# A gate's logits with the weights stationary and a group's features moving

## The chip, the cores and the metric

The kernel runs on one core of one Trainium2 chip. Its time is the device time of one execution in microseconds, the median of several runs. The core has five engines that matter here: TensorE (PE; its weight loads have rows of their own, PEld), VectorE (DVE), ScalarE (ACT), GpSimd (POOL), and SyncE (SP), which only issues transfers.

## The reference, cut to what matters

One layer of a graph network over 3125 nodes with 512 features. A two-layer graph attention and a linear attention are added to the input; then comes a mixture of eight experts of which each node uses two. The change touches the logits of the expert gate alone.

```python
def _L0_ffn_ref(x, Wg, bg, W1, b1, W2, b2):
    ...
    logits = xf @ Wg + bg
    probs = jax.nn.softmax(logits, axis=-1)
    _, top_idx = jax.lax.top_k(probs, TOP_K)
    mask = jnp.any(top_idx[:, :, None] == jnp.arange(NUM_EXPERTS)[None, None, :], axis=1)
    comb = probs * mask.astype(probs.dtype)
    out = jnp.zeros_like(xf)
    for e in range(NUM_EXPERTS):
        h = jax.nn.gelu(xf @ W1[e] + b1[e])
        y = h @ W2[e] + b2[e]
        out = out + comb[:, e:e + 1] * y
...
x = x + _L0_ffn_ref(_layernorm(x, axis=-1)[None], L0_ffn_Wg, ...)[0]
```

`xf` is 3125 x 512, `Wg` is 512 x 8, `W1[e]` is 512 x 128, `W2[e]` is 128 x 512, all in float32.

## The kernel before, in words

The two attention layers fill most of the time. After them, `last` (line 981) does the layer norms, the gate and the experts. Its nodes come in 25 tiles of 128 (`TILES`; the last one has 53), and these in seven groups of four tiles (`FGROUPS`; the last group is the tile of 53 alone). The group of 53 is first, then the other one that stayed on the chip (`STAY`; its features appear as `xg` in the profile), then the five others (`xT`).

For a group, the generator `gates(t0, k)` (line 987) makes the routing weights in steps divided by `yield`:

- `ps`, lines 998 to 1003: features turned to rows of nodes (TensorE), copied into `yall` by ScalarE, row statistics on VectorE.
- lines 1005 to 1021: first layer norm, the sum with `bt` and `bx`, which GpSimd gathers from memory, and statistics again.
- lines 1023 to 1035: the second layer norm gives `z`; `to_features` (line 450) turns `z` to features in four transposes into one PSUM tile `tr` (two buffers), and copies it into `xT` by VectorE and ScalarE in turn (lines 446 and 448). Then, tile by tile, the gate's product: four matmuls (one per chunk of 128 features, `NP` = 4) with the features of 128 nodes stationary and the 8 columns of `wgt` moving, into `pg` of 128 x 8 (PSUM, one buffer). VectorE adds the bias `bgt`, which is spread over 128 partitions, and writes `prob` (line 1035).
- lines 1038 to 1058: softmax over the 8 experts and a ranking, on VectorE but for one Exp on ScalarE.
- lines 1060 to 1066: the weights turned to `combT` (line 1063; `pc` shares the buffer of `pg`).

`expert_sums(t0, k, ahead)` (line 1068) uses them: `pb` (line 1074) has the second biases, then for each of eight experts `ph` (line 1080, four chunks of 512 columns), a Gelu on ScalarE into `hT` (line 1083), `py` (line 1087, four tiles) and a multiply-add into `yall` on VectorE (line 1089). After each expert it takes one step of the next group's `gates` (line 1091), so that the gate of a group is made in the time of the group before. At its end the rows go to memory through GpSimd's queue (line 1095). The first group's gate runs ahead of everything.

The program's order gives each instruction its priority; the order in which an engine takes them is set when the kernel is built, by which of them can be ready. In every engine they then run in that order. A float32 matmul appears as two instructions in the profile, a transpose as one.

`load_experts` (line 964) loads the experts' weights, `wgt`, `bgt` and `gt` on SP's queue, while the last attention layer ends.

Of the kernel before, what the change touches and what calls it, by code (L numbers as in the profile page):

```python
# [8 lines left out]
F32 = mybir.dt.float32  # L9
BF16 = mybir.dt.bfloat16  # L10
I32 = mybir.dt.int32
AF = mybir.ActivationFunctionType
# [9 lines left out]
NP = H // 2  # L22
# [4 lines left out]
NX = 8  # L27
FX = 128
GT = 4
# [4 lines left out]
P = 128  # L34
# [43 lines left out]
def rows_by_partition(ap, r0, n):  # L78

    return bass.AP(tensor=ap.tensor, offset=ap.offset + r0 * ap.shape[-1],  # L80
                   ap=[[0, n], [1, ap.shape[-1]]])
# [328 lines left out]
def listed_layers(ctx: ExitStack, tc: tile.TileContext, rows,  # L410
# [4 lines left out]
    nc = tc.nc  # L415
# [34 lines left out]
    def to_features(pool, tag, o, rows_sb, n, copy=None):  # L450

        ps = pool.tile([128, 512], F32, name="tr", tag=tag)
        for c in range(NP):
            nc.tensor.transpose(ps[:, c * n:(c + 1) * n], rows_sb[:n, c * 128:(c + 1) * 128],
                                ident[:n, :n])
        (copy or evacuate)(o, ps[:, :NP * n].rearrange("p (c r) -> p c r", c=NP))
# [8 lines left out]
    def row_stats(pool, rows_in, mv_t):  # L465
        n = rows_in.shape[0]
        st = pool.tile([P, 6], F32, name="row_st", tag="row_st", bufs=4)
        nc.vector.bn_stats(st[:n], rows_in)
        nc.vector.bn_aggr(mv_t, st[:n])

    def node(t):
        return rec[:TILES[t][1], t, 0:1]
# [491 lines left out]
    def load_experts(fp):  # L964
        w1t = fp.tile([128, NX, NP, FX], F32, name="w1t")
        w2t = fp.tile([FX, NX, D], F32, name="w2t")
        for e in range(NX):
            nc.sync.dma_start(w1t[:, e], w1[e].rearrange("(c p) f -> p c f", p=128))
            nc.sync.dma_start(w2t[:, e, :], w2[e])
        b2t = fp.tile([NX, D], F32, name="b2t")  # L970
        nc.sync.dma_start(b2t, b2)
        wgt = fp.tile([128, NP, NX], F32, name="wgt")
        nc.sync.dma_start(wgt, wg.rearrange("(c p) e -> p c e", p=128))
        bgt = fp.tile([P, NX], F32, name="bgt")
        nc.sync.dma_start(bgt, rows_by_partition(bg, 0, P))
        gt = fp.tile([P, D], F32, name="gt")
        nc.sync.dma_start(gt, rows_by_partition(rows, ROW_G, P))
        return w1t, w2t, b2t, wgt, bgt, gt


    def last(xT, w1t, w2t, b2t, wgt, bgt, gt):
        with tc.tile_pool(name="fin", bufs=1, reuse_waits="tile") as fp, \
# [4 lines left out]
            def gates(t0, k):  # L987


                tiles = TILES[t0:t0 + k]  # L990
                mv = fp.tile([P, GT, 2], F32, name="mv1", bufs=2)
                mv2 = fp.tile([P, GT, 2], F32, name="mv2", bufs=2)
                prob = fp.tile([P, GT, NX], F32, name="prob", bufs=3)
                nc.vector.memset(mv, 1.0)
                nc.vector.memset(mv2, 1.0)
                nc.vector.memset(prob, 0.0)
                for i, (t, n) in enumerate(tiles):
                    ps = pp.tile([P, 512], F32, name="ps", tag="tr")
                    for c in range(NP):
                        nc.tensor.transpose(ps[:n, c * 128:(c + 1) * 128],  # L1000
                                            xT[:, c, t * P:t * P + n], ident)
                    nc.scalar.copy(yall[:n, t, :], ps[:n])
                    row_stats(fp, yall[:n, t, :], mv[:n, i, :])
                yield
                inv = fp.tile([P, GT], F32, name="sd_y", bufs=2)
                nc.scalar.activation(inv, mv[:, :, 1], AF.Sqrt, bias=epst)
                nc.vector.reciprocal(inv, inv)
                for i, (t, n) in enumerate(tiles):
                    bt = fp.tile([P, D], F32, name="bt", bufs=4)
                    bx = fp.tile([P, D], F32, name="bx", bufs=3)  # L1010
                    for o, held_in in ((bt, base), (bx, xb)):
                        nc.gpsimd.indirect_dma_start(  # L1012
                            out=o[:n], out_offset=None, in_=held_in[:, :],
                            in_offset=bass.IndirectOffsetOnAxis(ap=node(t), axis=0))
                    nc.gpsimd.tensor_add(bt[:n], bt[:n], bx[:n])
                    y = yall[:n, t, :]
                    nc.vector.scalar_tensor_tensor(y, y, mv[:n, i, 0:1], gt[:n],
                                                   op0=OP.subtract, op1=OP.mult)
                    nc.vector.scalar_tensor_tensor(y, y, inv[:n, i:i + 1], bt[:n],  # L1019
                                                   op0=OP.mult, op1=OP.add)  # L1020
                    row_stats(fp, y, mv2[:n, i, :])
                yield
                sd = fp.tile([P, GT], F32, name="sd_z", bufs=2)
                nc.scalar.activation(sd, mv2[:, :, 1], AF.Sqrt, bias=epst)
                nc.vector.reciprocal(sd, sd)
                for i, (t, n) in enumerate(tiles):
                    z = fp.tile([P, D], F32, name="z", bufs=3)
                    nc.vector.tensor_scalar(z[:n], yall[:n, t, :], mv2[:n, i, 0:1], sd[:n, i:i + 1],
                                            op0=OP.subtract, op1=OP.mult)
                    to_features(pp, "tr", xT[:, :, t * P:t * P + n], z, n)  # L1030
                    pg = pp.tile([P, NX], F32, name="pg", bufs=1)
                    for c in range(NP):
                        nc.tensor.matmul(pg[:n], lhsT=xT[:, c, t * P:t * P + n], rhs=wgt[:, c, :],  # L1033
                                         start=(c == 0), stop=(c == NP - 1))
                    nc.vector.tensor_add(prob[:n, i, :], pg[:n], bgt[:n])
                yield

                m = fp.tile([P, GT], F32, name="pm", bufs=2)
                wide = [P, GT, NX]
                nc.vector.tensor_reduce(m, prob, AX.X, OP.max)  # L1040
                nc.vector.tensor_sub(prob, prob, m[:, :, None].to_broadcast(wide))
                nc.scalar.activation(prob, prob, AF.Exp)
                nc.vector.tensor_reduce(m, prob, AX.X, OP.add)
                nc.vector.reciprocal(m, m)
                nc.vector.tensor_mul(prob, prob, m[:, :, None].to_broadcast(wide))

                rank = fp.tile(wide, F32, name="rank", bufs=2)
                nc.vector.memset(rank, 0.0)
                for e in range(NX):
                    more = fp.tile(wide, F32, name="more", bufs=2)  # L1050
                    pe = prob[:, :, e:e + 1]
                    nc.vector.tensor_tensor(more[:, :, :e + 1], pe.to_broadcast([P, GT, e + 1]),
                                            prob[:, :, :e + 1], OP.is_gt)
                    if e + 1 < NX:
                        nc.vector.tensor_tensor(more[:, :, e + 1:], pe.to_broadcast([P, GT, NX - 1 - e]),
                                                prob[:, :, e + 1:], OP.is_ge)
                    nc.vector.tensor_add(rank, rank, more)
                nc.vector.scalar_tensor_tensor(prob, rank, 1.5, prob, op0=OP.is_lt, op1=OP.mult)
                yield
                combT = fp.tile([NX, GT * P], F32, name="combT", bufs=2)  # L1060
                pc = pp.tile([NX, 512], F32, name="pc", tag="pg", bufs=1)
                for i, (t, n) in enumerate(tiles):
                    nc.tensor.transpose(pc[:, i * P:i * P + n], prob[:n, i, :], ident[:n, :n])
                w = (k - 1) * P + tiles[-1][1]
                nc.vector.tensor_copy(combT[:, :w], pc[:, :w])
                gated[t0] = prob, combT

# [33 lines left out]
            for _ in gates(*groups[0]):  # L1101
                pass
            for i, g in enumerate(groups):
                expert_sums(*g, gates(*groups[i + 1]) if i + 1 < len(groups) else iter(()))
# [3 lines left out]
    for l in range(L):  # L1108
# [10 lines left out]
        with tc.tile_pool(name=f"x{l}", bufs=1, reuse_waits="tile") as fx:  # L1119
            parts = [stay[g] if g in STAY else fx.tile([128, NP, GT * P], F32, name=f"xT{g}")  # L1120
                     for g in range(len(FGROUPS))]
            xT = Groups(parts)
# [601 lines left out]
```

## Time and profile before

| what | us |
|---|---|
| median of the 3 runs shown (2830.23, 2837.37, 2837.75) | 2837.37 |
| the profiled execution | 2804.75 |
| its span, first to last instruction | 2803.0 |
| PE busy in the span | 2398.1 (86%) |
| DVE busy | 2054.1 (73%) |
| ACT busy | 1406.5 (50%) |
| POOL busy | 1414.4 (50%) |
| mean granted TensorE clock | 0.911 of full |

`last` begins at about 2321 us of the span. PE in the span's last five stretches of a hundred:

| stretch | PE busy | clock |
|---|---|---|
| 2300 to 2400 | 76.79 | 0.73 |
| 2400 to 2500 | 99.36 | 0.98 |
| 2500 to 2600 | 99.93 | 0.95 |
| 2600 to 2700 | 99.85 | 0.98 |
| 2700 to 2803 | 92.44 | 0.94 |

A line of the profile's groups gives line, engine, operation, the tiles written and read, the shape (for TensorE: rows times columns of the stationary operand, then the moving one), the count, and then busy time and the mean of one. In a timeline a line has the start, the time from the first start to the last end, and what ran. The end of a matmul is modelled and lies behind the start of the next, so what TensorE pays for a run of matmuls is the distance from its start to the start of what follows. "Clock" is the share of TensorE's full clock that the chip granted.

### The profile page before, as it was taken

To read this page: it belongs to the slowest core of one execution; us is meant where nothing else is said; L and a number is where in the kernel's file an instruction comes from. 1 tells how busy PE (TensorE), PEld (TensorE's weight loads), DVE (VectorE), ACT (ScalarE), POOL (GpSimd) and SP (SyncE) were. 2 spreads that over 40 slices of the span, in tenths; PEclk is the share of its full clock that TensorE was granted. 3 is DMA by queue.
4 is the path that set the end of the run, shared out by engine and by line. 5 is a ranking of instruction groups with operands and counts; after the bars stand their busy time and mean duration, and the time that the engine had idled before them with its cause. 6 is when DMAs were issued, how large, how long until landed. Compare 5 with 4: busy or idle time off the path is not lost. (4 is left out here: it accounts for less than half of the span.)

```text
span 2803.0 us, 30800 instructions
## 1 busy us (share of the span) xinstructions
PE 2398.1 (86%) x8935; PEld 1302.4 (46%) x8935; DVE 2054.1 (73%) x3186; ACT 1406.5 (50%) x5315; POOL 1414.4 (50%) x1153
## 2 busy tenths in 40 slices
PE   6987989889889876999697787979888486999998
PEld 3442445545455543344344555555555344444443
DVE  7810999999999985500679888989988566666663
ACT  1111568787776763200276767776767423222220
POOL 3362778888777770011657766676765323222100
PEclk9998999999999987999798888989999796999999
DMA  8434999999999984321869888989887441111000
GB/s 287 171 121 138 328 331 337 332 330 338 330 326 325 332 266 159 122 108 78 286 234 335 287 299 292 329 303 331 309 307 269 131 135 51 34 48 48 32 19 20
DMA packets 214478, 620.58 MB, mean 221 GB/s; under 512 B 48068, under 2 KB 53569, under 8 KB 210199
## 3 DMA queue, kind: packets, MB, share of 16 engines
q0 software_dynamic: 161696, 518.18, 52.4%
q1 hardware_dynamic: 50048, 95.36, 9.4%
q10 hardware_dynamic: 2556, 4.97, 0.5%
q8 instruction: 75, 1.23, 0.2%
q14 instruction: 103, 0.84, 0.1%
HBM read 543.80 MB, written 74.75 MB: 221 GB/s over the span
## 5 line engine op out<-in xcount | busy, mean ns | idle before, releaser
L583 POOL DMA_INDIRECT lane<-kvd,idx x906 | 1147.7, 1267 | 526.7 <-issue 179.7
L624 ACT ACTIVATE lane<-lane,sc 128x64 f32<-128x64 f32 x3888 | 945.4, 339 | 117.9 <-DVE sc L614 117.6
L588 DVE TENSOR_TENSOR lane<-lane,q 128x1024 f32<-128x1024 f32 (+1 forms) x464 | 549.0, 1193 | 161.8 <-DMA lane<-kvd,idx 146.7
L644 PE MATMUL agg<-ident,lane 128*128 128x128 f32 (+1 forms) x3272 | 531.6, 301 | 140.5 <-DVE lane L627 59.5
L644 PEld LDWEIGHTS agg<-ident,lane 128*128 128x128 f32 (+1 forms) x3272 | 424.2, 154 | 316.1 <-ACT lane L624 143.5
L589 DVE TENSOR_REDUCE sc<-lane 128x16 f32<-128x1024 f32 (+1 forms) x464 | 545.5, 1187 | 2.6 <-ACT lane L624 1.6
L627 DVE TENSOR_TENSOR lane<-lane,sc 128x1024 f32<-128x1024 f32 (+1 forms) x214 | 252.3, 1197 | 0.1
L1089 DVE SCALAR_TENSOR_TENSOR yall<-py,prob,yall 128x512 f32<-128x512 f32 (+1 forms) x200 | 148.8, 748 | 112.4 <-PE py L1087 100.8
L555 PE MATMUL pq<-wq,xg 128*128 128x512 f32 (+1 forms) x400 | 201.7, 634 | 18.5 <-ACT kt L734 12.2
L701 PE MATMUL po<-aT,wo 128*128 128x512 f32 (+1 forms) x448 | 194.2, 572 | 20.3 <-ACT aT L688 13.4
L1087 PE MATMUL py<-w2t,hT 128*128 128x512 f32 (+1 forms) x400 | 188.7, 610 | 1.8 <-ACT hT L1083 0.8
L1080 PE MATMUL ph<-xT,w1t 128*128 128x512 f32 x320 | 156.3, 630 | 0.0
L1095 POOL DMA_INDIRECT out<-yall,rec x25 | 25.0, 1001 | 252.3 <-DVE yall L1089 247.4
L1083 ACT ACTIVATE hT<-ph,colt 128x512 f32<-128x512 f32 (+1 forms) x56 | 35.4, 633 | 211.0 <-PE ph L1080 210.8
L494 POOL DMA_INDIRECT kvd<-kv,rec x25 | 24.7, 989 | 222.8 <-DVE kv L491 216.8
L491 DVE COPY kv<-pv 128x512 f32<-128x512 f32 (+1 forms) x25 | 17.3, 692 | 153.4 <-PE pv L488 153.4
L701 PEld LDWEIGHTS po<-aT,wo 128*128 128x128 f32 x448 | 80.3, 202 | 97.9 <-issue 64.9
L1087 PEld LDWEIGHTS py<-w2t,hT 128*128 128x128 f32 (+1 forms) x400 | 71.9, 189 | 101.3 <-issue 69.0
L555 PEld LDWEIGHTS pq<-wq,xg 128*128 128x128 f32 (+1 forms) x400 | 73.4, 199 | 92.8 <-issue 68.3
L372 ACT COPY kv<-pkv 128x512 f32<-128x512 f32 (+1 forms) x50 | 29.2, 585 | 163.8 <-PE pkv L370 136.4
L1012 POOL DMA_INDIRECT bt<-base,rec x25 | 26.8, 1072 | 160.1 <-DVE yall L1019 150.3
L370 PE MATMUL pkv<-wk,xT 128*128 128x512 f32 (+1 forms) x200 | 100.7, 637 | 5.8 <-ACT kv L372 5.8
(264 smaller groups left out, 3288.4 us busy)
## 6 DMA issues: line engine op xcount, KB each, us to landing
lane<-kvd,idx POOLq DMA_INDIRECT x906, 6.3
kvd<-kv SPq DMA_DIRECT2D x24, 512.0 KB, 2.7
zT<-ztd SPq DMA_DIRECT2D x48, 256.0 KB, 5.3
xmid<-xg SPq DMA_DIRECT2D x10, 1024.0 KB, 5.7
xT<-xmid POOLq DMA_DIRECT2D x10, 1024.0 KB, 10.3
xr<-in_x SPq DMA_DIRECT2D x24, 256.0 KB, 3.9
xb<-xo SPq DMA_DIRECT2D x24, 256.0 KB, 5.6
zd<-z SPq DMA_DIRECT2D x24, 256.0 KB, 2.7
```

The lines of the kernel that those rows point to most:

```text
L370: nc.tensor.matmul(ps[:n], lhsT=xT[t][:, c, :n], rhs=wkv[name][:, c, :], start=(c == 0), stop=(c == NP - 1))
L555: nc.tensor.matmul(ps[:n], lhsT=of_place(t, c), rhs=wq[:, c, :], start=(c == 0), stop=False)
L583: gets.append(nc.gpsimd.indirect_dma_start(out=kv[:n, k, :], out_offset=None, in_=kvd[l][:, :], in_offset=bass.IndirectOffsetOnAxis(ap=idx ...
L588: nc.vector.tensor_mul(ks, ks, self.q[:n, None, :].to_broadcast([n, g, D]))
L589: nc.vector.tensor_reduce(self.sc[:n, :, j:j + g].rearrange("p h g -> p g h"), ks.rearrange("p g (h d) -> p g h d", h=H), AX.X, OP.add)
L624: nc.scalar.activation(v[:, k, h, :], v[:, k, h, :], AF.Copy, scale=self.sc[:n, h, j + k:j + k + 1])
L627: nc.vector.tensor_mul(v, v, self.sc[:n, :, j:j + g].rearrange("p h g -> p g h")[:, :, :, None] .to_broadcast([n, g, H, DH]))
L644: nc.tensor.matmul(self.agg[:, c * n:(c + 1) * n], lhsT=kv[:n, k, c * 128:(c + 1) * 128], rhs=ident[:n, :n], is_transpose=True, start=firs ...
L701: nc.tensor.matmul(ps[:, :w], lhsT=wo[:, kk, c * 128:(c + 1) * 128], rhs=aT[gi][:, kk, :w], start=(kk == 0), stop=(kk == NP - 1))
L1080: nc.tensor.matmul(ph[:, :w], lhsT=w1t[:, e, c, :], rhs=xT[:, c, gs], start=(c == 0), stop=(c == NP - 1))
L1087: nc.tensor.matmul(py[:n], lhsT=hT[:, i * P:i * P + n], rhs=w2t[:, e, :], start=True, stop=True)
L1089: nc.vector.scalar_tensor_tensor(yall[:n, t, :], py[:n], prob[:n, i, e:e + 1], yall[:n, t, :], op0=OP.mult, op1=OP.add)
```

## The change

The bias is loaded as one column of eight partitions. The gate's product leaves the loop over tiles and moves behind a `yield` of its own: four matmuls for the whole group, with the 8 columns of `wgt` stationary and up to 512 nodes moving, into `pg` of 8 x 512. ScalarE adds the bias on the way into the new tile `gin`. Up to four transposes turn `gin` back to rows of nodes in `pt`, in the buffer that `pg` and `pc` have, and VectorE copies them to `prob` (one copy for a group whose tiles are whole; the group of 53 has one tile and one copy).

```diff
-        bgt = fp.tile([P, NX], F32, name="bgt")
-        nc.sync.dma_start(bgt, rows_by_partition(bg, 0, P))
+        bgt = fp.tile([NX, 1], F32, name="bgt")
+        nc.sync.dma_start(bgt, bg.rearrange("o e -> e o"))
...
                     to_features(pp, "tr", xT[:, :, t * P:t * P + n], z, n)
-                    pg = pp.tile([P, NX], F32, name="pg", bufs=1)
-                    for c in range(NP):
-                        nc.tensor.matmul(pg[:n], lhsT=xT[:, c, t * P:t * P + n], rhs=wgt[:, c, :],
-                                         start=(c == 0), stop=(c == NP - 1))
-                    nc.vector.tensor_add(prob[:n, i, :], pg[:n], bgt[:n])
+                yield
+
+                gs = slice(t0 * P, t0 * P + (k - 1) * P + tiles[-1][1])
+                w = gs.stop - gs.start
+                pg = pp.tile([NX, 512], F32, name="pg", bufs=1)
+                for c in range(NP):
+                    nc.tensor.matmul(pg[:, :w], lhsT=wgt[:, c, :], rhs=xT[:, c, gs],
+                                     start=(c == 0), stop=(c == NP - 1))
+                gin = fp.tile([NX, GT * P], F32, name="gin", bufs=2)
+                nc.scalar.activation(gin[:, :w], pg[:, :w], AF.Identity, bias=bgt)
+                pt = pp.tile([P, GT, NX], F32, name="pt", tag="pg", bufs=1)
+                for i, (t, n) in enumerate(tiles):
+                    nc.tensor.transpose(pt[:n, i, :], gin[:, i * P:i * P + n], ident[:NX, :NX])
+                for n, i0, i1 in ((P, 0, k - 1), (tiles[-1][1], k - 1, k)) if tiles[-1][1] < P else ((P, 0, k),):
+                    if i1 > i0:
+                        nc.vector.tensor_copy(prob[:n, i0:i1, :], pt[:n, i0:i1, :])
                 yield
```

The line that set `w` for `combT` falls away, since `w` is known.

## The prediction

> **What bounds the kernel now.** The edit touches `last` alone, so I went from the page's slices (the last five of 40, from 2450 us on, have PE at 9 or 8) to the chain of waits of one period of it, then to busy time by stretch. The chain between 2452 and 2523 us, shares by line:
>
> ```profile
> by line: PE ph L1080 41.5%; PE py L1087 40.3%; PE pb L1074 8.4%; PE pg L1033 4.5%; PE tr L454 2.6%; PE ps L1000 1.4%; ACT hT L1083 1.0%; PE pc L1063 0.6%; issue 0.2%; ACTq L1083 0.0%
> ```
>
> Nearly all of it is TensorE, with the gate's L1033 at 4.5%. Busy time in two periods of a group (stretch, length; PE, PEld, DVE, ACT, POOL; clock, DMA share, GB/s):
>
> ```profile
> 2452.00:2521.00 69.00, 68.92 (x205) 33.09 (x206) 46.38 (x107) 17.22 (x23) 17.53 (x17) 0.98 0.14 47
> 2521.00:2590.00 69.00, 68.93 (x205) 33.13 (x206) 46.16 (x107) 17.22 (x23) 17.65 (x17) 0.98 0.15 47
> ```
>
> PE is busy 68.9 of 69 us, DVE 46, ACT 17. From 2390 us to the end the time is the sum of PE's slots, and only a change of slots or of the clock counts. Between 2319 and 2390 us it is different: PE waits (idle 2363 to 2366.5), and the clock is mostly 0.50.
>
> **Change part by part.** There are seven gates: one of 53 nodes (group 1, before everything), one of 512 in the short period of group 1 (group 2), five of 512 in dense periods. PE's timeline in a dense one:
>
> ```profile
> 2484.32 0.95 PE L1033 MATMUL pg<-wgt,xT 128*128 128x8 f32 x8
> 2485.13 0.64 PE L454 MATMUL tr<-ident,z 128*128 128x128 f32 x4
> 2485.60 1.02 PE L1087 MATMUL py<-w2t,hT 128*128 128x512 f32 x2
> 2486.46 0.95 PE L1033 MATMUL pg<-wgt,xT 128*128 128x8 f32 x8
> ```
>
> Slots go from start to start: eight pg 0.81 us (0.10 each), four tr 0.47, two py 0.86 (0.43 each).
>
> *Removed:* 4 x 0.81 = 3.24 us of PE in a dense gate. *Added:* four products of width 512, two instructions each as for L1080 (64 for one group's 8 experts x 4 chunks), 8 x 0.43 = 3.44. No row has a stationary 8 wide with a stream of 512; the nearest for the width is L1063:
>
> ```profile
> 2387.58 0.60 PE L1063 MATMUL pc<-ident,prob 128*8 128x128 f32 x4
> 2388.02 0.82 PE L1000 MATMUL ps<-ident,xT 128*128 128x128 f32 x6
> ```
>
> Four with an 8-wide stationary take 0.44 us, against 0.47 for tr at 128 wide: width buys at most 6%. Bounds 3.23 (0.94 x 3.44) and 3.63 (eight pb in the chain); I take 3.44, since the stream is as long as L1080's. The four turns (8 rows, 128 wide, stream of 8) aren't in the trace: pg at 0.10 is bound by the same 128-wide load, tr at 0.12 is above, half of pg below. I take 0.40 (0.20 to 0.47). A dense gate: 3.44 + 0.40 - 3.24 = +0.60 (+0.2 to +0.9); five: **+3.0 us** (+1.0 to +4.3).
>
> [...]
>
> *ScalarE and VectorE.* Groups by line, 2330 us to the end:
>
> ```profile
> L1083 ACT ACTIVATE hT<-ph,colt 128x512 f32<-128x512 f32 x48 | 33.0, 687 | 203.8 <-PE ph L1080 203.7
> L1035 DVE TENSOR_TENSOR prob<-pg,bgt 128x8 f32<-128x8 f32 x24 | 4.0, 167 | 11.9 <-PE pg L1033 11.3
> ```
>
> `gin` is an ACTIVATE over 512 columns, 0.69 us by the first row. Identity (L935) and Relu (L954) have no table load in the groups, so none is added. ACT has 52 us free in 69. Four adds of 0.17 on DVE become one copy of about 0.17. Neither is on the path: cost 0 while PE has other products. The new wait: the turns stand on PE behind `gin`, and py and ph behind the turns. Uncovered, that is 0.69 for `gin`, 0.14 by which pg's end lies behind its slot and 0.04 until its reader starts, 5 x 0.9 = +4.5 us. But PE fills such holes now (it lost 0.1 us before all 160 dense pg), so **+0.5** (0 to +4.5). Behind `gin` on ACT stand the next hT and Exp's table load; the hT comes from a ph behind pg anyway. Logits come up to 2 us later in a dense gate, and what L1063 turns then lies some 20 us until L1074, which hides that; if L1074 came at once it would be 2 us a gate. `pt` shares the one buffer of pg and pc; the next pg is some 50 us behind pc's copy, so nothing waits for it.
>
> *Group 1* isn't dense: its chain gains `gin` at 53 columns (0.31 by the narrow hT), a turn (0.25 by L1063's narrow form) and up to 1.0 from Exp's table load, which now falls behind `gin`. VectorE ends L1058 at 2345.3 and L1063 starts at 2347.96, after 16 ph. That 2.6 us covers it: **0** (0 to +1.5). The bias load is one small transfer at 2270.6 on SP, 66 us ahead of use; `gt` behind it is used at 2330.7: 0. The added yield moves only priorities: 0.
>
> *Group 2 and the clock.* Stretches of one clock step (steps lie on a grid of 3.41 us; columns as above):
>
> ```profile
> 2350.10:2353.50 3.40, 3.40 (x5) 0.88 (x5) 2.54 (x5) 1.09 (x1) 0.00 (x0) 0.50 0.00 0
> 2353.50:2356.90 3.40, 3.40 (x16) 1.74 (x15) 3.29 (x7) 0.95 (x4) 1.72 (x2) 1.00 0.27 77
> 2360.30:2363.70 3.40, 2.25 (x5) 0.34 (x4) 3.31 (x8) 1.20 (x2) 2.98 (x3) 1.00 0.42 113
> ...
> 2370.60:2373.90 3.30, 3.30 (x18) 3.30 (x17) 0.86 (x2) 0.47 (x1) 2.73 (x3) 0.50 0.24 74
> ...
> 2380.90:2384.20 3.30, 3.30 (x6) 1.14 (x5) 2.15 (x19) 0.00 (x0) 0.00 (x0) 0.50 0.00 0
> 2384.30:2387.60 3.30, 3.30 (x14) 1.60 (x13) 0.86 (x3) 2.88 (x4) 0.00 (x0) 1.00 0.00 0
> ...
> 2452.50:2455.90 3.40, 3.40 (x9) 1.33 (x8) 2.67 (x6) 0.00 (x0) 2.18 (x3) 1.00 0.48 183
> 2455.90:2459.30 3.40, 3.40 (x5) 1.35 (x4) 0.41 (x1) 0.00 (x0) 0.00 (x0) 0.50 0.18 69
> ```
>
> At 2452.5 PE is fully busy with pb, 8 rows of stationary, and the next step is at 0.50. At 2370.6 it is fully busy with pg and tr, mostly loads, and stays at 0.50 until a step full of ph. So I counted, over all steps, the time in which columns stream, weighted by the rows they use (K/128). Of 619 steps at full clock, 54 are followed by 0.50, with shares up to 0.37; the 565 others start at 0.37. The 54 that bring the clock back start at 0.75. Weighted by columns of the stationary as well, the rule breaks: 2350.1 (py, 53 wide: rows 0.91, cells 0.38) brings the clock back, and 2360.3 (rows 0.50, cells 0.21) keeps it. So rows seem to count and width doesn't. [...]
>
> Now group 2 spends 6.43 us in 32 pg slots at half clock that hardly stream (shares 0.39 to 0.60 from 2367 to 2381), and reaches full clock at 2384.23. Afterwards, once the fourth tile is out of PSUM (about 2370.8), eight streams fill the steps; the first full one ends between 2374.2 and 2377.6. Full clock comes some 8 us sooner, worth 4 us of PE work. Against it: 0.6 more slots and some 0.9 waiting for the fourth tile. VectorE's ranking (4.3 us after the logits, 2378.9 to 2383.2) then fits under the 16 ph. Net -2.5 to -3.5, I take **-3.0**. Bounds: -4.5 with a lucky phase; +2.3 with no earlier clock (8 x 0.86 + 0.8 - 6.43 = +1.25, and 1 of waiting).
>
> **Sum:** +3.0 + 0.5 + 0 - 3.0 = +0.5 us on the profiled execution's 2804.75 (span 2803.0 and 1.75 around it). That is 32.6 us, 1.1%, under the median of the runs shown, 2837.37; I carry the difference over: 2838.
>
> **Rivals.**
> *Width counts for the clock after all* (slower). Nothing narrower than 53 streams for long in this trace, and eight may be another matter. For: pb, as sparse in cells (1/16), halves the clock every time. Against: the two 53-wide steps. Place: the steps after pg in the dense gates. It decides once more than some 63% of a step is pg, which 3.44 us in steps of 3.41 do in about three phases of four. Price: pb's six dips last 3.41 us four times and 6.83 twice, mean 4.55, half of it lost, 2.3; four gates 9.1. Group 2 is then +1.3. Sum 3.0 + 0.5 + 9.1 + 1.3 = +14: **2851**.
> *The head shrinks further* (faster). If group 2's whole half-clock stretch (17.07 us from 2367.16) falls away, that is -8.5, and if the order also fills the idle 3.3 us before it, 3.0 + 0.5 - 8.5 - 3.3 = -8.3, in the best phase -9: **2828**. For: PE is 77% busy there. Against: that idle time ends on z of L1028, which comes from gathers and VectorE, untouched.
> *PE waits for `gin` in each dense gate* and the early clock is partly lost: 3.0 + 4.5 + 0 = +7.5 to +9: **2846**. Against: the filling seen now.
> *It does no more than swap equal slots*, phases of the clock deciding: within my forecast.
>
> **How the numbers follow.** Chances: forecast 0.50, width 0.27, head 0.13, wait 0.10. A measurement of this kernel can tell about 0.3%, 8.5 us, from no change. Slower: width 0.25 (with all but its mildest form), half of the wait 0.05, the forecast's tail 0.03, 0.33. Faster: the head 0.13 and 0.02 of tail, 0.15. The rest, 0.52, is within. The forecast alone spans 2833 to 2845; the range is taken out to both ends, 2829 to 2852.
>
> **What would show it.** Right: eight L1033 slots of 0.43 in a row in a dense gate, four turns of about 0.1, dense periods 0.6 us longer, clock 1.00 right after pg, dips only after pb, and full clock before 2378 in group 2. Wrong: 0.50 in the step after pg (width counts); PE idle before the turns (the wait); slots far from 0.43; group 2's first pb not earlier against its first z.

## The result and the profile after

| | median, us | lowest to highest | runs |
|---|---|---|---|
| before, on the same chip | 2832.76 | 2825.5 to 2845.13 | 12 |
| after | 2833.28 | 2820.53 to 2839.72 | 12 |

The ratio is 0.9993 (95%: 0.9976 to 1.001): no change that can be told, -2.0 us with an interval of -6.8 to +2.8 (the two medians alone differ by +0.5).

The profiled execution took 2835.68 us, its span 2833.9, against 2803.0 before. All of this lies ahead of the edit: `last` starts (first `ps`) at 2321.16 us before and at 2356.81 after, 35.65 later, and up to there both kernels run the same instructions, in the same order but for two neighbours on VectorE early in the span. So `last` is compared from its own start, cut at each group's first `pb` (starts from PE's timeline; the first group is that of 53 nodes, group 2 the next):

| us | before | after |
|---|---|---|
| start of `last` to the first pb (group 1) | 27.34 | 27.68 |
| to group 2's pb | 41.12 | 35.28 |
| the next five, with a dense gate each | 339.70 | 339.99 |
| last pb to the last matmul | 63.95 | 64.42 |
| start of `last` to the end of the span | 481.86 | 477.14 |

The chain of waits over one period after, shares by line:

```profile
by line: PE py L1097 42.4%; PE ph L1090 41.2%; PE pb L1084 5.3%; PE pg L1037 5.2%; PE tr L454 2.6%; PE ps L1000 1.4%; ACT hT L1093 1.0%; PE pc L1074 0.6%; PE pt L1043 0.5%; issue 0.2%; ACTq L1093 0.0%
```

`pg` went from 4.5% to 5.2%, and the new `pt` has 0.5%. `pb` fell from 8.4% to 5.3% without having been touched: this period has no fall of the clock behind `pb`, the one shown of before had one. Two such periods (stretch, length; PE, PEld, DVE, ACT, POOL busy; clock, DMA share, GB/s):

```profile
2552.30:2620.30 68.00, 67.93 (x185) 29.79 (x184) 45.82 (x104) 17.89 (x24) 17.49 (x17) 1.00 0.15 47
2620.30:2688.30 68.00, 67.93 (x185) 29.79 (x184) 46.12 (x101) 17.89 (x24) 14.40 (x14) 1.00 0.11 35
```

They are 1 us shorter than before's 69.0, and at clock 1.00 instead of 0.98. That comes from where the falls of the clock lie and not from the edit: before's two periods have a fall of 3.41 us each, these have none, and without any fall a period of the old form takes 67.26 (experiment 4). The dense gate in PE's timeline (start, time to the last end, what ran):

```profile
2446.90 3.60 PE L1097 MATMUL py<-w2t,hT 128*128 128x512 f32 x8
2450.43 3.60 PE L1037 MATMUL pg<-xT,wgt 128*8 128x512 f32 x8
2453.96 1.12 PE L1090 MATMUL ph<-xg,w1t 128*128 128x512 f32 x2
2455.02 0.41 PE L1043 MATMUL pt<-ident,gin 8*128 8x8 f32 x4
2455.36 4.56 PE L1090 MATMUL ph<-xg,w1t 128*128 128x512 f32 x10
```

From start to start the eight `pg` take 3.53 us (0.44 each) and the four turns 0.34 (0.085 each). The two `ph` between take 1.06 where 0.86 is their price, so PE loses 0.2 us ahead of the turns. What is late there is `gin`. The groups by shape over 2360 us to the end, and the list of waits over 2400 to 2720 (engine, what waited, for what: us, times, longest):

```profile
L1040 ACT ACTIVATE gin<-pg,bgt 8x512 f32<-8x512 f32 x6 | 4.1, 678 | 32.2 <-PE pg L1037 32.2
L1043 PE MATMUL pt<-ident,gin 8*128 8x8 f32 x24 | 2.5, 207 | 0.0
L1043 PEld LDWEIGHTS pt<-ident,gin 8*128 8x128 f32 x24 | 1.9, 136 | 4.5 <-ACT gin L1040 4.5
```

```profile
PEld pt L1043 <- ACT gin L1040: 3.8, 5, 0.8
```

The load of the turns stands 0.8 us behind `gin` (0.68), but the two `ph` queued ahead of it cover most of that; only the 0.2 reach PE.

Clock steps in the dense periods (columns as above):

```profile
2451.80:2455.20 3.40, 3.40 (x11) 0.77 (x9) 0.00 (x0) 1.11 (x2) 0.00 (x0) 1.00 0.10 39
2455.30:2458.60 3.30, 3.30 (x11) 1.61 (x10) 2.60 (x21) 2.94 (x4) 0.00 (x0) 1.00 0.00 0
...
2482.60:2485.90 3.30, 3.30 (x9) 1.15 (x7) 2.64 (x5) 0.00 (x0) 2.43 (x3) 1.00 0.55 210
2486.00:2489.30 3.30, 3.30 (x4) 1.32 (x5) 0.66 (x1) 0.00 (x0) 0.00 (x0) 0.50 0.21 79
```

In the first step 2.23 of 3.40 us are `pg`, with a stationary 8 columns wide, and the next step is at 1.00. In the third it is `pb`, 8 rows, and the next is at 0.50. So here half clock followed the 8 rows and not the 8 columns; experiments 3 and 4 test each alone. Behind `pb` the clock was at half for 20.5 us in this execution (after four of the six `pb` of whole groups) and for 27.3 in the one before (after all six), each with 6.83 of it behind the last `pb`, and that is why the five dense periods above differ by only 0.3.

Group 2 before, PE's timeline (in brackets the idle time ahead and what ended it) and two clock steps:

```profile
2366.55 1.41 PE L454 MATMUL tr<-ident,z 128*128 128x128 f32 x8 [3.32 <-DVE z L1028]
...
2389.63 3.70 PE L1074 MATMUL pb<-b2t,combT 8*128 8x512 f32 x8
```

```profile
2363.80:2367.10 3.30, 0.55 (x5) 0.54 (x6) 3.14 (x6) 0.00 (x0) 3.06 (x3) 1.00 0.37 113
2367.20:2370.50 3.30, 3.15 (x15) 2.75 (x14) 1.71 (x5) 0.59 (x1) 1.75 (x3) 0.50 0.53 158
```

Group 2 after:

```profile
2401.68 1.08 PE L454 MATMUL tr<-ident,z 128*128 128x128 f32 x8 [3.05 <-DVE z L1028]
...
2405.36 0.63 PE L454 MATMUL tr<-ident,z 128*128 128x128 f32 x4 [1.46 <-DVE mv L995]
2406.00 0.55 PE L1000 MATMUL ps<-ident,xT 128*128 128x128 f32 x3
2406.66 3.60 PE L1037 MATMUL pg<-xg,wgt 128*8 128x512 f32 x8
...
2419.78 3.69 PE L1084 MATMUL pb<-b2t,combT 8*128 8x512 f32 x8
```

```profile
2400.60:2404.00 3.40, 1.74 (x12) 1.25 (x12) 3.40 (x5) 0.58 (x1) 2.92 (x4) 1.00 0.28 81
2404.00:2407.40 3.40, 1.91 (x9) 0.92 (x10) 1.93 (x4) 0.58 (x1) 2.83 (x3) 1.00 0.45 118
2407.50:2410.80 3.30, 3.30 (x9) 0.75 (x7) 0.00 (x0) 0.50 (x1) 0.53 (x1) 1.00 0.20 47
```

PE waits for z and again ahead of the fourth tile's transposes, and yet the clock stays at 1.00 throughout; before, it was at 0.50 for 17.07 us here. From the first transpose to `pb` it takes 18.10 us, against 23.08 before.

### The profile page after: what moved, and what is told of

Same layout as the page of the kernel before. It is cut to its first block, busy times and chain, and to the rows that moved or that the text cites. A ratio compares the mean times of both kernels' runs of the same rounds, so it can differ in the third digit from the quotient of the medians.

```text
span 2833.9 us, 30554 instructions
## 1 busy us (share of the span) xinstructions
PE 2402.8 (85%) x8816; PEld 1281.2 (45%) x8816; DVE 2052.4 (72%) x3168; ACT 1411.5 (50%) x5323; POOL 1397.0 (49%) x1153
## 5 line engine op out<-in xcount | busy, mean ns | idle before, releaser
L583 POOL DMA_INDIRECT lane<-kvd,idx x906 | 1127.4, 1244 | 561.9 <-issue 225.3
L644 PEld LDWEIGHTS agg<-ident,lane 128*128 128x128 f32 (+1 forms) x3272 | 418.0, 153 | 323.9 <-issue 134.4
L701 PE MATMUL po<-aT,wo 128*128 128x512 f32 (+1 forms) x448 | 201.8, 592 | 28.5 <-ACT aT L688 13.8
L720 PE MATMUL pq<-wmp,mqT 128*128 128x512 f32 (+1 forms) x200 | 100.2, 644 | 9.0 <-ACT mqT L843 7.0
L720 PE MATMUL pq<-wmk,zT 128*128 128x512 f32 (+1 forms) x200 | 99.4, 616 | 6.3 <-ACT kt L734 2.7
```

Source lines behind the costliest of these rows:

```text
L583: gets.append(nc.gpsimd.indirect_dma_start(out=kv[:n, k, :], out_offset=None, in_=kvd[l][:, :], in_offset=bass.IndirectOffsetOnAxis(ap=idx ...
L644: nc.tensor.matmul(self.agg[:, c * n:(c + 1) * n], lhsT=kv[:n, k, c * 128:(c + 1) * 128], rhs=ident[:n, :n], is_transpose=True, start=firs ...
L701: nc.tensor.matmul(ps[:, :w], lhsT=wo[:, kk, c * 128:(c + 1) * 128], rhs=aT[gi][:, kk, :w], start=(kk == 0), stop=(kk == NP - 1))
L720: nc.tensor.matmul(ps[:n], lhsT=lhs(c), rhs=w[:, c, :], start=(c == 0), stop=(c == NP - 1 and bias is None))
```

## The experiments

Theory: the dense gates cost what their slots say (+3.5 us in five), group 2 gains because the clock is full sooner, and what halves the clock is streaming through few rows of the stationary, not few columns. Rivals: width counts for the clock; group 2's gain comes from the order of the work and not from the product's form; or it is the clock's phase alone.

The table has each profiled execution from its own start of `last`, cut as above, and the time at half clock that began in group 2's stretch ahead of its `pb`. It is the base of all readings below; the times of whole runs follow with each experiment. The kernel before had medians of 2801.07 (13 runs) beside experiments 1 to 4, and 2799.62 (17 runs) beside 5 to 8.

| us | group 1 | group 2 | five dense | last | to the end | half clock, group 2 |
|---|---|---|---|---|---|---|
| before | 27.34 | 41.12 | 339.70 | 63.95 | 481.86 | 17.07 |
| after | 27.68 | 35.28 | 339.99 | 64.42 | 477.14 | 0 |
| e1 group 2 old | 27.69 | 40.30 | 344.37 | 60.80 | 482.87 | 17.07 |
| e2 dense gates old | 27.68 | 35.30 | 339.57 | 64.10 | 476.39 | 0 |
| e3 product twice | 28.38 | 40.59 | 360.98 | 64.36 | 504.07 | 6.83 |
| e4 before, pb with 64 rows | 27.33 | 39.60 | 329.70 | 60.80 | 467.15 | 13.65 |
| e5 before, pb with 32 rows | 27.35 | 39.61 | 338.06 | 62.49 | 477.22 | 13.65 |
| e6 after, pb with 64 rows | 27.69 | 35.28 | 333.44 | 60.80 | 466.91 | 0 |
| e7 group 2 alone new, 64 rows | 27.34 | 35.46 | 329.76 | 60.80 | 463.08 | 3.41 |
| e8 before, one more step | 27.34 | 41.25 | 338.09 | 62.30 | 478.66 | 17.07 |

### 1. The old product in group 2 alone

```diff
+                grouped = t0 != 20
...
+                    if not grouped:
+                        pg = pp.tile([P, NX], F32, name="pg", bufs=1)
+                        for c in range(NP):
+                            nc.tensor.matmul(pg[:n], lhsT=xT[:, c, t * P:t * P + n], rhs=wgt[:, c, :], ...)
+                        nc.vector.tensor_add(prob[:n, i, :], pg[:n], bgr[:n])
...
+                if grouped:
+                    yield
...
```

`bgr` is the bias spread over 128 partitions, loaded beside the column. Tile 20 begins group 2.

> Group 2's gate (the first of 512 nodes) goes tile by tile as before, the other six as in the change. Theory (rows of the stationary count for the clock, a dense gate costs its stream): the dense periods without a clock dip stay at 68.0 us, as in the change, and the stretch from the first pb to the second goes back from 35.3 to some 41 us if the clock falls to 0.50 in it, with full clock only some 5 us after the last of the 32 small products. Rival (the 5.8 us of group 2 came from another order of gathers and from the phase of the clock's steps, not from the streams): the stretch stays at 35 to 37 us.

Measured: 40.30 us in group 2 (after 35.28), 17.07 of them at half clock; 2799.39 in one run, which tells nothing by itself.

```profile
2359.59 1.08 PE L454 MATMUL tr<-ident,z 128*128 128x128 f32 x8 [2.03 <-DVE z L1032]
2361.15 1.88 PE L1038 MATMUL pg<-wgt,xg 128*128 128x8 f32 x8 [0.48 <-DVE xg L448]
...
2370.17 1.71 PE L1038 MATMUL pg<-wgt,xg 128*128 128x8 f32 x8
2371.73 5.47 PE L1101 MATMUL ph<-xg,w1t 128*128 128x512 f32 x6
...
2382.70 3.69 PE L1095 MATMUL pb<-b2t,combT 8*128 8x512 f32 x8
```

From the first transpose to `pb` (PE's timeline) it is 23.11 us again, with the pg slots at 1.57 us for each of the last three tiles, nearly twice the 0.81 of full clock. The five dense periods are long here (344.37) for the falls behind `pb`: 23.9 us at half clock, against 20.5 after, of which 6.83 lay behind the last `pb` and so in none of the five. Group 2's gain belongs to group 2's own gate.

### 2. The old product in the five dense gates

The same edit with `grouped = t0 >= 20`. Group 1's gate is in the new form here too, with group 2's; only the five dense ones are old. The expectation has group 1's gate in the old form, which isn't what the edit does.

> Group 1 and the five dense gates go tile by tile as before, group 2's gate as in the change. Theory: dense periods without a dip are 67.3 us, 0.7 less than in the change, and the stretch from the first pb to the second is at most 38 us: if the clock falls before group 2, it is back within 7 us of the start of the 8-wide stream. Rival (order and phase): group 2's stretch is anywhere between 35 and 41 us and, where the clock has fallen, it isn't back before the dense ph products.

Measured: group 2 35.30 us, as after, and no fall of the clock there; five dense periods 339.57, end 476.39, which is 5.5 under before. One run took 2799.14. So the gain is there without the dense gates. It does not refute the rival by itself: 35.30 lies in the rival's range too, and the clock did not fall. The 67.3 us of a period could not be read, since a fall lies in each. Their own cost does not show between 339.57 and 339.99, since both hold falls behind `pb`; that takes experiments 4 and 6.

### 3. The group's product done twice

```diff
-                for c in range(NP):
+                for c in [*range(NP), *range(NP)]:
```

> The change with the gate's product done twice in each gate (the second pass overwrites the first). Theory: each dense gate costs 8 more slots of 0.44, so +3.5 us in each of five periods and about the same in group 2, together +18 to +21 us (ratio to before 1.006 to 1.008), and the clock stays at 1.00 through 7 us of 8-wide streams. Rival (width counts): the clock falls to 0.50 in the step after each, another 1.7 to 3.4 us a gate, together +27 to +38 us (1.010 to 1.013).

Measured: 2824.92 (4 runs), ratio 1.0086 (1.006 to 1.0112). A dense gate's sixteen `pg` lie between 2417.35 and 2424.32 us: two clock steps that are almost `pg` alone, and the one after:

```profile
2417.35 7.03 PE L1037 MATMUL pg<-xT,wgt 128*8 128x512 f32 x16
```

```profile
2417.80:2421.20 3.40, 3.40 (x9) 0.71 (x8) 0.41 (x1) 0.00 (x0) 0.00 (x0) 1.00 0.27 77
2421.20:2424.60 3.40, 3.40 (x9) 0.83 (x8) 0.00 (x0) 0.18 (x1) 0.00 (x0) 1.00 0.00 0
2424.60:2428.00 3.40, 3.40 (x12) 1.42 (x12) 1.67 (x12) 3.09 (x4) 0.00 (x0) 1.00 0.00 0
```

7 us of an 8-wide stationary leave the clock at 1.00, in every dense gate of this trace. The rival of the width falls by this. The times don't decide: the ratio lies between the theory's 1.006 to 1.008 and the rival's 1.010 to 1.013, and its interval reaches into both. The five dense periods are 21.0 longer than after, 17.5 of it the second passes (five of 3.5). The half clock behind `pb` is 27.3 us instead of 20.5, and half of that difference is the other 3.4. In group 2 the clock fell here for 6.83 us; less the second pass the stretch is 37.1, between the 35.3 of no fall and the 40.4 of the old form.

### 4. pb with 64 rows, on the kernel before

```diff
-        b2t = fp.tile([NX, D], F32, name="b2t")
-        nc.sync.dma_start(b2t, b2)
+        b2t = fp.tile([64, D], F32, name="b2t")
+        nc.vector.memset(b2t, 0.0)
+        nc.sync.dma_start(b2t[:NX], b2)
...
+            combs = [fp.tile([64, GT * P], F32, name=f"combT{i}") for i in range(2)]
+            for o in combs:
+                nc.vector.memset(o, 0.0)
...
-                combT = fp.tile([NX, GT * P], F32, name="combT", bufs=2)
+                combs.reverse()
+                combT = combs[0]
...
-                nc.vector.tensor_copy(combT[:, :w], pc[:, :w])
+                nc.vector.tensor_copy(combT[:NX, :w], pc[:, :w])
```

56 of the 64 rows are zero, so the sum is the same; only the rows in use change.

> The kernel before, with the stationary of pb (and the biases under it) filled up with zero rows from 8 to 64; the gate is as before. Theory (the clock falls where rows in use times streaming time is under some 3/8 of a step): 64 rows of 128 is 0.5, so no step after pb is at 0.50; that takes away 3 to 6 dips of 1.7 to 3.4 us: -6 to -13 us (ratio 0.995 to 0.998), pb's own slots unchanged at 0.45. Rival (what counts is data that isn't zero, or the load of the biases): the dips stay, ratio 1.000.

Measured: 2782.97 (8 runs), ratio 0.9947 (0.9929 to 0.9966), -14.9 us, a little more than the -6 to -13 forecast (`last` alone: 467.15 against 481.86). `pb` has the same slot as with 8 rows, 3.62 us for eight, and no fall of the clock follows any of them:

```profile
2576.23 3.70 PE L1079 MATMUL pb<-b2t,combT 64*128 64x512 f32 x8
2579.85 2.84 PE L1085 MATMUL ph<-xT,w1t 128*128 128x512 f32 x6
```

```profile
2441.60:2509.00 67.40, 67.33 (x206) 32.44 (x205) 46.56 (x107) 17.22 (x23) 17.53 (x17) 1.00 0.15 48
2509.00:2576.20 67.20, 67.13 (x205) 32.44 (x204) 46.08 (x106) 17.22 (x23) 17.46 (x17) 1.00 0.15 47
```

With PE as busy as before (67.33 us of 67.40, against 68.92 of 69.00), only the rows differ, and 56 rows of zeros were enough to keep the clock at 1.00. It also gives the old form's period without a fall, 67.26 us. How busy the profile shows PE does not tell the two apart: in before's step at 2452.5 PE is busy 3.40 of 3.40 us, with 8 rows, and the next step is at 0.50; here the step at 2576.2 has 3.40 of 3.40 too, with 64 rows, and the next is at 1.00.

### 5. The same with 32 rows

> As the 64-row kernel, but pb's stationary filled up to 32 rows only (a quarter of 128). Theory (rows in use times streaming time against 3/8 of a step): a step that is nearly all pb counts 0.25 and halves the clock, one that pb shares with ph or py (over some 17% of it) counts 0.37 or more and doesn't; pb takes 3.6 us against a step of 3.41, so few or none of the six groups dip, 0 to 3, against 6 in the trace of before. Rival (any row of a block of 32 counts for the block, so that 8 rows are counted as 32 already): four to six dips as before.

Measured: 2796.57 in one run; the clock fell behind five of the six `pb`. That is more than the forecast's 0 to 3; by number it is the rival's four to six. Two steps with `pb`, each with the step after it; the first stayed, the second fell:

```profile
2515.00:2518.40 3.40, 3.40 (x9) 1.33 (x8) 2.80 (x6) 0.00 (x0) 2.49 (x4) 1.00 0.40 154
2518.40:2521.80 3.40, 3.40 (x9) 1.29 (x8) 1.55 (x3) 0.00 (x0) 0.87 (x1) 1.00 0.40 154
2583.30:2586.70 3.40, 3.40 (x8) 1.23 (x8) 2.83 (x5) 0.00 (x0) 2.61 (x3) 1.00 0.59 225
2586.70:2590.00 3.30, 3.30 (x5) 1.51 (x5) 0.69 (x1) 0.00 (x0) 0.00 (x0) 0.50 0.21 82
```

By my count of streaming time times K/128, the step that stayed has 0.41 and the five that fell 0.24 to 0.33. I had taken it that `pb`, being longer than a step, would mostly share its steps with `ph` or `py`; in the five that fell it fills 0.8 of a step or more by this count. That rows might be counted in blocks of 32 is contradicted: a step of the kernel before with 8-row `pb` fell at a share of 0.36 (the step ahead of the fall at 2394.5), which blocks would make 0.47, and 0.41 stayed here.

### 6. pb with 64 rows, on the changed kernel

The edit of experiment 4 on the kernel after.

> The change with pb's stationary filled up to 64 rows. Theory: no dip after pb and none after the gate's product; five dense periods of 68.0 us, 0.75 above those of the 64-row kernel alone (67.26), a stretch of 35 to 38 us from the first pb to the second against 39.6: together 0 to -1 us against that kernel, ratio to before 0.993 to 0.997. Rival (the 8-wide streams do cost clock once pb doesn't): periods over 69.5 us, ratio 0.997 to 1.002.

Measured: 2787.18 (12 runs), ratio to before 0.9952 (0.9934 to 0.997). No fall in group 2 or behind `pb`:

```profile
2436.10:2504.20 68.10, 68.03 (x185) 29.73 (x184) 46.00 (x104) 17.90 (x24) 17.47 (x17) 1.00 0.15 47
2504.20:2572.20 68.00, 67.93 (x185) 29.81 (x184) 45.51 (x104) 17.89 (x24) 17.50 (x17) 1.00 0.15 47
```

Here a dense gate's price can be read, because no fall hides it: 68.0 against 67.26 in experiment 4. Over the five periods 333.44 - 329.70 = +3.7 us.

### 7. The best of both: group 2 alone in the new form, pb with 64 rows

`grouped = t0 == 20`, as in experiment 1's edit, with the edit of experiment 4: groups 1 and 3 to 7 as before.

> The gate as in the change for group 2 alone, tile by tile elsewhere, and pb's stationary filled up to 64 rows. Theory (terms add): dense periods 67.3 us, group 2's stretch 35 to 38 us, no dips: 2 to 4 us under the 64-row kernel, ratio to before 0.992 to 0.995. Rival (order and phase): like the 64-row kernel, 0.9947.

Measured: 2779.68 (6 runs), ratio 0.993 (0.9905 to 0.9955), -19.6 us: faster than the kernel before. In `last` it is 3.8 us shorter than experiment 6 and 4.1 shorter than experiment 4; the runs' times can't tell it from experiment 4, since the rival's 0.9947 lies in the interval. The parts add up in the trace: dense periods of 67.27 as in experiment 4, group 2 at 35.46 as after, nothing behind `pb`. The clock did fall in group 2 here, but for 3.41 us only.

### 8. The added step alone

```diff
                         nc.vector.tensor_add(prob[:n, i, :], pg[:n], bgt[:n])
                 yield
+                yield
```

This is the kernel before with one more step behind the gate's products, as the change has it.

> The kernel before with the added step (yield) behind the gate's product and nothing else. It separates the change of order from the change of the product. Theory (streams): group 2's stretch stays at 39.6 to 41.1 us with the clock at 0.50 for 13 to 17 us from z on. Rival (the step alone gives another order of the gathers and of the products): 35 to 37 us, and no long fall of the clock before group 2.

Measured: group 2 41.25 us (before 41.12; a little over the forecast's 41.1), 17.07 at half clock, 2809.18 in one run.

```profile
2374.30 1.28 PE L454 MATMUL tr<-ident,z 128*128 128x128 f32 x8 [3.30 <-DVE z L1028]
...
2384.88 1.72 PE L1033 MATMUL pg<-wgt,xg 128*128 128x8 f32 x8
...
2397.37 2.84 PE L1075 MATMUL pb<-b2t,combT 8*128 8x512 f32 x6
```

```profile
2371.60:2375.00 3.40, 0.70 (x7) 0.69 (x7) 3.29 (x6) 0.00 (x0) 3.20 (x3) 1.00 0.33 107
2375.00:2378.40 3.40, 3.11 (x16) 2.72 (x15) 1.67 (x5) 0.58 (x1) 1.91 (x2) 0.51 0.52 154
```

One step with PE at 0.70 of 3.40 us, and the next is at half. From the first transpose to `pb` it is 23.07 us, as in experiment 1. So the added step gives nothing by itself. What gives it is the rest of the change: the product moved behind all four tiles, with its operands' roles exchanged. Those two were not run apart.

## Why the prediction came out, point by point

**The total.** Forecast +0.5 us, measured -2.0 (-6.8 to +2.8): no change to be told, as forecast. That 2838 lies 4.7 over the median is almost all base: before itself had 2837.37 in the runs shown and 2832.76 in twelve. The stated range also holds before's own 2832.76, so the total could not have told this sum from no effect at all. Nor does it tell of the steps, since two of opposite sign cancel; the terms had to be measured one by one.

**The slots of a dense gate: right.** Eight `pg` took 3.53 (forecast 3.44, bounds 3.23 and 3.63), the turns 0.34 (0.40). The bounds from L1063 and from `pb` held, with 0.44 for each f32 instruction.

**The wait for `gin`: right in kind, somewhat over the value taken.** 0.2 us a gate, 1.0 for five, against 0.5 forecast and 4.5 at most; two `ph` fill the rest. The rival that PE waits in each gate (0.9) is refuted. Slots and wait together were put at +3.5, and experiments 4 and 6 give +3.7 (the timeline's 0.29 + 0.34 + 0.20 a gate gives 4.2; the half microsecond between them was not traced).

**Group 1: +0.34** instead of 0, within the bound of 1.5.

**Group 2: the mechanism right, the size wrong.** This is the term that failed: -3.0, with a bound of -4.5. Five runs with the old form had 41.12, 40.30, 39.60, 39.61 and 41.25 us (mean 40.4), four with the new one 35.28, 35.30, 35.28 and 35.46 (mean 35.3): -5.05. The step was "full clock comes some 8 us sooner". It came 10 to 17 us sooner: the half clock of 17.07 or 13.65 us shrank to 3.41 or to nothing. I had taken the fall ahead of group 2 as given and only let it end sooner. In three of the four it never came, and in the fourth (experiment 7) it lasted 3.41 us and the stretch was only 0.2 us longer. That it never came may be partly luck of the phase: by my count the two steps ahead of the product, from 2397.2 and 2400.6 us, have 0.37 and 0.38, where the falls in the traces of before and after reach up to 0.36, the second from twelve transposes in a row that the product no longer parts; in experiment 7 the like step had 0.35 and the clock fell. In the step from 2404.0 us shown above, `pg` streams for the last 0.75 us; my count gives that step 0.44, of which `pg` is 0.22. Without it the step would be well under that 0.36. That this stream is what held the clock there is worked out, not shown, since the order around it can't be kept without it.

**The rivals.** "The head shrinks further" had half of it: the stretch at half clock did fall away, but the price of -8.5 left out what its own new form adds there: 0.29 of slots, 0.34 of turns, 0.2 for `gin` and 1.46 for the fourth tile, 2.3 together; -6.2 is near the -5.84 of the profiled pair. Its other half, that the idle time before z is filled, didn't happen (3.05 us after). "Width counts" is refuted by experiment 3 and by every dense gate: the clock is at 1.00 in the step after each `pg` there. "Equal slots, phases of the clock deciding" is true of a single execution: the falls behind `pb` summed to 27.3 us in one and 20.5 in the other, worth 3.4 us, as much as all five dense gates cost.

**The sum** of the measured terms, 3.7 - 5.05 + 0.34 = -1.0, against +0.5 forecast.

**What stays open.** Whether the clock falls at all ahead of group 2 may depend on how PE's idle time (2.0 to 3.3 us, before z) lies against the steps of 3.41 us. The old form fell in five of five, the new one in two of five (experiments 3 and 7), and shortly. How much of that is the form and how much the phase was not separated. The length at half clock sets the two forms apart in every run: 13.65 or 17.07 us in the old form, at most 6.83 in the new one. Nor was the old product run behind all four tiles at once, so how much of the gain comes from bunching the products and how much from the long stream through 8 columns is open.

The forecast counted 619 steps at full clock, 54 of them followed by half. That is what the trace holds from about 200 to 2790 us; over its whole span the same count gives 667 and 59, with the same bound of 0.37.

## What to carry to other kernels

Ask of a matmul how many rows of the stationary its stream uses, not only how long PE is busy. Here eight `pb` with 8 rows, 3.62 us against a clock step of 3.41, were followed by half clock behind six of six in the trace of before; padded with zero rows to 64 they were followed by none, which was worth 14.9 us (experiment 4), more than the whole change. Where a change has a part in dense stretches and a part where an engine waits, price and test them apart: here one lost 3.7 us, the other won 5, and the version that kept only the second took 0.7% off together with the padding, which alone took 0.5%. A zero in the total is no proof that nothing happened.

## What the runs showed of the chip that was not expected

- Rows of zeros were enough to keep the clock: `pb` with 8 rows of data and 56 of zeros kept 1.00 (experiments 4 and 6), in the same 3.62 us in which 8 rows led to half clock for 3.41 to 6.83 us (behind six of six `pb` before, behind four of six after).
- A narrow stationary did not cost it: 7 us of streams through one 8 columns wide, with all 128 rows, left the clock at 1.00 (experiment 3).
- My count, the share of streaming time in a step weighted by K/128, parted the steps at full clock in the trace of before: the largest share with half clock behind it is 0.363, the smallest with full clock behind it 0.368. In the trace of after the two overlap a little: a step with 0.355 (from 2158.3 us) kept full clock, one with 0.363 (from 1752.1 us) lost it. The count describes these two traces; how the chip decides was not shown.
- A turn of 8 rows by 128 took 0.085 us of PE, less than the 0.12 of a 128 x 128 one (`tr` before); an ACTIVATE on 8 partitions with 512 columns took 0.68 us (`gin` after), as long as one on 128 (`hT`, 0.69).
